# Adding lam for the large block's last stage one step ahead, in a kernel of two attention layers

## The chip, the cores and the metric

The kernel runs on one core of a Trainium2 chip. The metric is the device time of one execution in microseconds (us), from first to last instruction plus a small launch share. Engines go by their short names: PE is the matrix engine (PEld its weight load), DVE the vector engine, ACT the scalar (activation) engine, POOL the GpSimd engine, SP the engine whose queue issues the DMAs.

## The reference, cut to what matters

The input x is 8 batches of 512 tokens with 128 features. Two parts follow each other, each adding to x. Only the first part bears on this change:

```python
s = einsum(Q, K) * scale                       # 16 heads of 8 features, causal
lam = max(where(mask, s, -1e30)) + 1.0         # one lam per query and head
for _ in range(4):                             # NUM_ITER Newton steps
    d = maximum(lam - s, EPS)
    f  = sum(1/d over the mask) - 1.0
    fp = -sum(1/d**2 over the mask)
    lam = lam - f / fp
p = 1 / maximum(lam - s, EPS), masked, divided by its sum
o = p @ V                                      # then o @ Wo.T, added to x
```

So each query's lam grows in four steps, each of which passes over all its scores, and a last pass with the final lam gives the weights that multiply V. The second part is six layers of windowed attention with a feed-forward net; the change does not touch its code.

## The kernel before, in words

**Blocks and pairs.** The 512 queries of a batch are cut into four blocks of 128. Block rb sees (rb + 1) * 128 keys, and its four 32-row pieces see between that less 96 and that, so a tile has 4W - 192 columns for W = (rb + 1) * 128: 320, 832, 1344, 1856 for rb 0 to 3. Each block holds 16 heads, worked on in four groups j. Blocks go in pairs, a large one (index u = 0) and a small one (u = 1): (3, 0), then (2, 1), for each of the 8 batches; the list `work` (L384) has 16 pairs.

**Three pairs at once.** The loop over w (L391) holds a pair `before` whose lam is final, a pair `now` that is in its Newton steps, and a pair `nxt` whose scores are made. Stage w has four steps k. In each step, for u = 0 and 1:

- `attend_add(before[u], k)` (L317): POOL adds the final lam to the scores of head group k, in four instructions (L263, tile `da`, one per row piece). The tile comes from the pool `dl_p`, which has three buffers, so an add may write only when the transposes (L338) of the tile three adds earlier have read it.
- `scores(nxt[u], k)` (L237): PE makes the scores (L248) and DVE moves them into the tile `ns` of that block and group (L253). That tile has one buffer per block number and group, so DVE may write it only after the `attend_add` that read the same buffer two stages back in the pair sequence, that is `attend_add(before[u], k)`.
- `newton(now[u], k)` (L283): for the large block ACT computes ln(lam + ns) with lam as its bias (L297) and exp(-...) (L298) and DVE sums with statistics (L300). For the small block POOL adds lam first, in `add_lams(now[1])` (L275, L399), four tiles `df` of four instructions each (L263), then ACT takes ln and exp (L293, L298). A short chain on DVE (L304, L306, L308, L310, L313, L314, L315) then gives the new lam.
- `attend_weigh(before[u])` (L322): ACT takes ln (L324) and exp (L325) of the tile `da`.
- `attend_sum` of the tile weighed just ahead (L327): PE transposes it (L338), DVE applies the mask (L341, tile dT), PE multiplies with V (L350), DVE copies the sum (L354). With the last group, `attend_end` follows (L362): transposes (L366), a division (L370), a transpose (L375), an ACT copy oT (L377), a matmul (L379) and DVE's add to x (L380). After block rb 1 the batch's x is complete and `normalized_T` (L88) makes its normalized transpose: statistics (L93, L94), rstd on ACT (L96, L97), `xn` on DVE (L101, four instructions), transposes (L105), an ACT copy xT (L106).

After every second stage `project` (L190) prepares the batch after next: a `normalized_T` again (same lines, copy xnT), query, key and value projections (L196 to L214), and two POOL memsets of the value tile (L206, L207).

**What sets the order.** Every engine runs its own list of instructions strictly in order; an instruction that waits holds up all behind it on its engine. The lists are not the order of the source: a scheduler in the build step works through the program by priority (earlier in the source is higher) and by its own estimate of when operands and buffers are there, so source order is only a wish.

Of the kernel before, what the change touches and what calls it, by code (L numbers as in the profile page):

```python
# [25 lines left out]
NUM_ITER = 4  # L26
# [24 lines left out]
def tile_kernel(  # L51
# [57 lines left out]
    with ExitStack() as c1:  # L109
# [119 lines left out]
        def block(b, rb, proj):  # L229

            W = (rb + 1) * P
            return dict(
                b=b, x=xs[b], rb=rb, W=W, proj=proj, ns=[None] * 4, nkb=rb + 1,
                mn=sm.tile([P, H], F32, name="mn"), lam=sm.tile([P, H], F32, name="lam"), o4=None,
            )

        def scores(t, j):  # L237

            rb, W, (qj, kn, va) = t["rb"], t["W"], t["proj"]
            sp = sp_a if rb in (0, 3) else sp_b  # L240
            ns = t["ns"][j] = sp.tile([P, 4 * W - 6 * Q], F32, name="ns", tag=f"ns{rb}{j}")
            nv = pieces(ns, W)
            s = [ps_s.tile([P, W], F32, name="s", tag="s") for a in range(4)]
            for a in range(4):
                q0 = rb * P + a * Q
                for g in range(4):
                    rows = slice(32 * g, 32 * g + 32)
                    nc.tensor.matmul(  # L248
                        s[a][rows, 0 : keys(W, a)], lhsT=qj[rows, j, q0 : q0 + Q],
                        rhs=kn[rows, 0 : keys(W, a)], start=True, stop=True,  # L250
                    )
            for a in range(4):
                nc.vector.tensor_tensor_reduce(  # L253
                    nv[a], s[a][:, 0 : keys(W, a)], far[:, N - keys(W, a) : N],
                    1.0, 3e38, ALU.add, ALU.min, t["mn"][:, 4 * j + a : 4 * j + a + 1],
                )

        def add_lam(t, d, j):

            W = t["W"]  # L260
            for a, (o, n) in enumerate(zip(pieces(d, W), pieces(t["ns"][j], W))):
                by = t["lam"][:, 4 * j + a : 4 * j + a + 1]
                nc.gpsimd.tensor_tensor(o, n, by.to_broadcast([P, keys(W, a)]), ALU.add)  # L263

        def first_lam(t):
            lam, mn = t["lam"], t["mn"]


            nc.vector.tensor_scalar(lam, mn, -1.0, 1.0, ALU.mult, ALU.add)
            for e in (2.0**-21, -(2.0**-21)):  # L270
                nc.vector.scalar_tensor_tensor(
                    lam, mn, -1.0 - e, lam, ALU.mult, ALU.max
                )

        def add_lams(t):  # L275

            t["df"] = []
            for j in range(4):
                d = dp.tile([P, 4 * t["W"] - 6 * Q], F32, name="df", bufs=4)
                add_lam(t, d, j)  # L280
                t["df"].append(d)

        def newton(t, k):  # L283
            W, lam = t["W"], t["lam"]

            st = sm.tile([P, H, 2, 3], F32, name="stw")
            for j in range(4):
                ns = t["ns"][j]
                few = W <= 2 * P
                d = t["df"][j] if few else dp.tile([P, 4 * W - 6 * Q], F32, name="d")  # L290
                dv, nv = pieces(d, W), pieces(ns, W)
                if few:
                    nc.scalar.activation(d, d, AF.Ln)  # L293
                else:
                    for a in range(4):
                        c = 4 * j + a
                        nc.scalar.activation(dv[a], nv[a], AF.Ln, bias=lam[:, c : c + 1])  # L297
                nc.scalar.activation(d, d, AF.Exp, scale=-1.0)  # L298
                for a in range(4):
                    nc.vector.bn_stats(st[:, 4 * j + a].rearrange("p u k -> p (u k)"), dv[a])  # L300

            mean = st[:, :, :, 1]
            s1 = sm.tile([P, H, 2], F32, name="s1")
            nc.vector.tensor_tensor(s1, mean, st[:, :, :, 0], ALU.mult)  # L304
            q2 = st[:, :, :, 0]
            nc.vector.tensor_tensor(q2, s1, mean, ALU.mult)  # L306
            sw2 = sm.tile([P, H], F32, name="sw2")
            nc.vector.tensor_reduce(sw2, st[:, :, :, 0:3:2], axis=AX.XY, op=ALU.add)  # L308
            sw = sm.tile([P, H], F32, name="sw")
            nc.vector.scalar_tensor_tensor(  # L310
                sw, s1[:, :, 0], -1.0, s1[:, :, 1], ALU.add, ALU.add
            )
            nc.vector.reciprocal(sw2, sw2)  # L313
            nc.vector.tensor_tensor(sw, sw, sw2, ALU.mult)  # L314
            nc.vector.scalar_tensor_tensor(lam, sw, 0.0, lam, ALU.max, ALU.add)  # L315

        def attend_add(t, j):  # L317

            d = t["d"] = dl_p.tile([P, 4 * t["W"] - 6 * Q], F32, name="da")
            add_lam(t, d, j)  # L320

        def attend_weigh(t):  # L322
            d = t["d"]
            nc.scalar.activation(d, d, AF.Ln)  # L324
            nc.scalar.activation(d, d, AF.Exp, scale=-1.0)  # L325

        def attend_sum(t, d, j):  # L327

            nkb, W, (qj, kn, va) = t["nkb"], t["W"], t["proj"]
            if j == 0:  # L330
                t["o4"] = bt.tile([P, 4, P], F32, name="o4")
            dT = tr.tile([P, nkb, 4, P], F32, name="dT", tag="dT")
            for a in range(4):

                d0 = sum(keys(W, c) for c in range(a))
                pt = ps_t.tile([P, nkb, P], F32, name="dTp", tag="t")
                for kb in range(nkb):
                    nc.tensor.transpose(  # L338
                        pt[:, kb, :], d[:, d0 + kb * P : d0 + (kb + 1) * P], ident
                    )  # L340
                nc.vector.tensor_tensor(  # L341
                    dT[:, :, a, :], pt,
                    seen[:, a, N - W : N].rearrange("p (b c) -> p b c", c=P), ALU.mult,
                )

            po = ps_o.tile([P, 4, Q], F32, name="po")
            for kb in range(nkb):
                for g in range(4):
                    rows = slice(32 * g, 32 * g + 32)
                    nc.tensor.matmul(  # L350
                        po[rows, :, :], lhsT=va[:, kb, 4 * g + j, :],
                        rhs=dT[:, kb, :, rows], start=(kb == 0), stop=(kb == nkb - 1),
                    )
            nc.vector.tensor_copy(t["o4"][:, j, :], po.rearrange("p a q -> p (a q)"))  # L354
            if j == 3:
                attend_end(t)
                if t["rb"] == 1:
                    b, xb = t["b"], t["x"]
                    normalized_T(bt, ps_m, xb, xT[:, b, :])
                    nc.sync.dma_start(x2[b].rearrange("(c p) d -> p c d", p=P), xb)  # L360
# [29 lines left out]
        now, before, ready = [], [], None  # L390
        for w in range(len(work) + 1):  # L391
            before, now, nxt = now, nxt, []
            if w + 1 < len(work):
                b, rbs = work[w + 1]
                nxt = [block(b, rb, proj) for rb in rbs]
            for t in now:
                first_lam(t)
            for k in range(NUM_ITER):
                if now:  # L399
                    add_lams(now[1])  # L400
                for u in range(2):
                    if before:
                        attend_add(before[u], k)
                    if nxt:
                        scores(nxt[u], k)
                    if now:
                        newton(now[u], k)
                    if ready:
                        attend_sum(*ready)
                        ready = None  # L410
                    if before:
                        attend_weigh(before[u])
                        ready = (before[u], before[u]["d"], k)
            if w + 2 < len(work) and work[w + 2][1][0] == 3:
                if ready:
                    attend_sum(*ready)
                    ready = None
                proj = project(work[w + 2][0])
# [511 lines left out]
```

## Time and profile before

The page covers one execution on core 0. "The first part" below is the stretch up to about 1675 us.

| what | value |
| --- | --- |
| median of 3 runs | 5099.98 us (5099.35 to 5100.96) |
| the profiled execution, its own time | 5104.72 us |
| its span, first to last instruction | 5102.8 us (1.9 us less) |
| busy over the span | PE 83%, DVE 80%, ACT 70%, POOL 58% |
| in 400 to 500 us | PE 67.8, DVE 88.6, ACT 94.4, POOL 47.9 us busy |
| in 500 to 600 us | PE 53.4, DVE 82.8, ACT 89.4, POOL 40.2 us busy |
| POOL's adds in the first part (L263) | df x1024, 396.9 us busy; da x512, 310.7 us busy |
| mean granted PE clock | 0.891 |

Rows of the timeline read: start in us from the span's start, length in us, engine, line, operation, output tile <- input tiles, shape, how many instructions are merged into the row, and in brackets how long the engine sat idle before it and what it was waiting for. The length of a merged row runs from the first start to the last end.

### The profile page before, as it was taken

To read this page: it belongs to the slowest core of one execution; us is meant where nothing else is said; L and a number is where in the kernel's file an instruction comes from. 1 tells how busy PE (TensorE), PEld (TensorE's weight loads), DVE (VectorE), ACT (ScalarE), POOL (GpSimd) and SP (SyncE) were. 2 spreads that over 40 slices of the span, in tenths; PEclk is the share of its full clock that TensorE was granted. 3 is DMA by queue.
4 is the path that set the end of the run, shared out by engine and by line. 5 is a ranking of instruction groups with operands and counts; after the bars stand their busy time and mean duration, and the time that the engine had idled before them with its cause. 6 is when DMAs were issued, how large, how long until landed. Compare 5 with 4: busy or idle time off the path is not lost.

```text
span 5102.8 us, 163213 instructions
## 1 busy us (share of the span) xinstructions
PE 4223.2 (83%) x67981; PEld 2494.8 (49%) x67981; DVE 4081.0 (80%) x11020; ACT 3561.4 (70%) x6314; POOL 2983.0 (58%) x3828
## 2 busy tenths in 40 slices
PE   4556556556554899999999999999999999999998
PEld 1233333223232556555555555565555555556554
DVE  7789888888887877877787778877787778778775
ACT  6889999999898565666666666666666566665664
POOL 2434444444345666666666666666666666666663
PEclk7667667667665999999999999999999999999999
DMA  0000000000001323232233322332323323233232
GB/s 9 1 5 1 5 5 1 5 3 3 3 1 26 69 63 73 58 81 62 60 74 71 67 65 61 76 73 59 70 59 81 69 56 73 63 76 76 62 75 48
DMA packets 273623, 240.73 MB, mean 47 GB/s; under 512 B 47056, under 2 KB 269048, under 8 KB 272888
## 3 DMA queue, kind: packets, MB, share of 16 engines
q1 hardware_dynamic: 272888, 230.30, 20.1%
q8 instruction: 538, 8.81, 0.7%
q14 instruction: 197, 1.61, 0.1%
HBM read 21.52 MB, written 4.19 MB: 5 GB/s over the span
## 4 chain that ended last, share of the span: by engine, by line
PE 43%; DVE 30%; ACT 19%; POOL 5%; issue 2%; DMA 0%; ACTq 0%; POOLq 0%; DVEq 0%; SPq 0%
PE m L555 9%; PE po L683 6%; DVE qr L571 5%; DVE ss L561 5%; ACT d L297 5%; DVE stw L300 5%; DVE qn L563 5%; PE pT L671 4%; PE acc L711 3%; PE ptq L625 3%; ACT d L298 3%; PE pv L591 3%; POOL da L263 2%; PE gp L761 2%; PE y L782 2%; PE s L645 2%
## 5 line engine op out<-in xcount | busy, mean ns | idle before, releaser
L575 POOL TENSOR_TENSOR qn<-qn,qr 128x512 f32<-128x512 f32 x768 | 978.0, 1274 | 1048.4 <-DVE qr L571 828.1
L583 POOL TENSOR_TENSOR qn<-qn,ss 128x512 f32<-128x512 f32 x768 | 785.8, 1044 | 58.4 <-ACT ss L580 58.4
L561 DVE TENSOR_REDUCE ss<-sq 128x8 f32<-128x512 f32 x768 | 521.9, 680 | 369.7 <-ACT sq L560 369.7
L263 POOL TENSOR_TENSOR df<-ns,lam 128x32 f32<-128x32 f32 (+7 forms) x1024 | 396.9, 425 | 608.9 <-DVE lam L315 393.4
L555 PE MATMUL m<-wqkv,xs 128*128 128x512 f32 x1536 | 726.6, 595 | 2.0 <-ACT v L595 1.7
L297 ACT ACTIVATE d<-ns,lam 128x416 f32<-128x416 f32 (+7 forms) x1024 | 559.4, 615 | 65.8 <-DVE stw L300 27.7
L560 ACT ACTIVATE sq<-m 128x512 f32<-128x512 f32 x768 | 459.7, 599 | 188.5 <-PE m L555 183.8
L571 DVE TENSOR_TENSOR qr<-m,tab 128x256 f32<-128x256 f32 x1536 | 572.0, 414 | 0.0
L300 DVE BATCH_NORM_STATS2 stw<-d 128x6 f32<-128x416 f32 (+7 forms) x1024 | 514.7, 561 | 55.3 <-ACT d L298 54.7
L248 PE MATMUL s<-kn,qj 32*32 32x160 f32 (+15 forms) x4096 | 426.0, 493 | 152.0 <-DVE mn L253 136.0
L630 ACT COPY qT<-ptq 128x512 f32<-128x512 f32 x768 | 419.9, 579 | 175.3 <-PE ptq L625 175.3
L338 PE MATMUL dTp<-ident,da 128*128 128x128 f32 x1280 | 297.4, 373 | 293.7 <-issue 67.0
L563 DVE TENSOR_TENSOR qn<-m,tab 128x512 f32<-128x512 f32 x768 | 522.0, 680 | 0.0
L263 POOL TENSOR_TENSOR da<-ns,lam 128x416 f32<-128x416 f32 (+15 forms) x512 | 310.7, 639 | 321.4 <-PE dTp L338 256.3
L625 PEld LDWEIGHTS ptq<-ident,qn 128*128 128x128 f32 x3072 | 359.7, 141 | 210.8 <-issue 146.8
L683 PE MATMUL po<-v,prT 64*32 64x65 f32 x24576 | 391.9, 224 | 77.5 <-DVE pr L650 77.4
L591 PE MATMUL pv<-wqkv,xs 128*128 128x512 f32 x768 | 431.6, 644 | 0.0
L656 POOL TENSOR_TENSOR pr<-pr,nm 128x512 f32<-128x512 f32 x384 | 400.9, 1044 | 20.2 <-DVE nm L655 20.2
L711 PE MATMUL acc<-oT,wo 128*128 128x512 f32 x768 | 397.6, 599 | 15.0 <-ACT oT L705 15.0
L338 PEld LDWEIGHTS dTp<-ident,da 128*128 128x128 f32 x1280 | 199.8, 187 | 421.3 <-issue 210.1
L625 PE MATMUL ptq<-ident,qn 128*128 128x128 f32 x3072 | 399.3, 273 | 7.1 <-DVE qr L571 3.6
L683 PEld LDWEIGHTS po<-v,prT 64*32 64x32 f32 x24576 | 324.5, 105 | 157.8 <-DVE pr L650 127.1
(139 smaller groups left out, 8211.7 us busy)
## 6 DMA issues: line engine op xcount, KB each, us to landing
v<-v SPq DMA_DIRECT2D x1152, 130.0 KB
v<-v SPq DMA_DIRECT2D x384, 97.5 KB
v<-v SPq DMA_DIRECT2D x192, 65.0 KB
wqkv<-in_L_ffn_Wqkv_dram SPq DMA_DIRECT2D x24, 256.0 KB
wqkv<-in_L_ffn_Wqkv_dram SPq DMA_DIRECT2D x24, 128.0 KB
wo<-in_L_ffn_Wo_dram SPq DMA_DIRECT2D x12, 256.0 KB
xb<-in_L_attn_x_dram SPq DMA_DIRECT2D x8, 256.0 KB
x<-xb SPq DMA_DIRECT2D x8, 256.0 KB
```

The source lines that it names most:

```text
L263: nc.gpsimd.tensor_tensor(o, n, by.to_broadcast([P, keys(W, a)]), ALU.add)
L297: nc.scalar.activation(dv[a], nv[a], AF.Ln, bias=lam[:, c : c + 1])
L300: nc.vector.bn_stats(st[:, 4 * j + a].rearrange("p u k -> p (u k)"), dv[a])
L555: nc.tensor.matmul(m.rearrange("p h e -> p (h e)"), lhsT=lhsT, rhs=wqkv[:, t, :], start=True, stop=True,)
L561: nc.vector.tensor_reduce(ss[:, t, :], sq, axis=AX.X, op=ALU.add)
L563: nc.vector.tensor_tensor(qc, m, tab[:, 2 * t, c, :].unsqueeze(1).to_broadcast([P, HH, DHL]), ALU.mult)
L571: nc.vector.tensor_tensor(qr[:, :, u, :], mh[:, :, 1 - u, :], sw.unsqueeze(1).to_broadcast([P, HH, hd]), ALU.mult,)
L575: nc.gpsimd.tensor_tensor(qc, qc, qr.rearrange("p h u e -> p h (u e)"), ALU.add)
L583: nc.gpsimd.tensor_tensor(qc, qc, ss[:, t, :].unsqueeze(2).to_broadcast([P, HH, DHL]), ALU.mult)
L591: nc.tensor.matmul(pv, lhsT=lhsT, rhs=wqkv[:, 2, :], start=True, stop=True,)
L625: nc.tensor.transpose(pt[:, c * P : (c + 1) * P], g["qn"][t][:, c, 2 * p : 2 * p + 2, :].rearrange("p h e -> p (h e)"), ident,)
L683: nc.tensor.matmul(po[u * QB : (u + 1) * QB, e, c, :], lhsT=prT[rows, c, u * QB : (u + 1) * QB], rhs=g["v3"][rows, n, p, :], start=True, s ...
```

## The change

`attend_add` for the large block of the finished pair moves from the head of its step to the end of the step ahead, so that in the source it stands in front of the next `add_lams`, which needs the new lam of the Newton step just made. For the first step of a stage it moves to the end of the stage ahead, where that pair is still called `now`. The small block's `attend_add` stays. No instruction is added or dropped.

```diff
@@ -399,7 +399,7 @@
                 if now:
                     add_lams(now[1])
                 for u in range(2):
-                    if before:
+                    if before and u:
                         attend_add(before[u], k)
                     if nxt:
                         scores(nxt[u], k)
@@ -411,6 +411,12 @@
                     if before:
                         attend_weigh(before[u])
                         ready = (before[u], before[u]["d"], k)
+
+                if k + 1 < NUM_ITER:
+                    if before:
+                        attend_add(before[0], k + 1)
+                elif now:
+                    attend_add(now[0], 0)
             if w + 2 < len(work) and work[w + 2][1][0] == 3:
                 if ready:
                     attend_sum(*ready)
```

## The prediction

> **What bounds the kernel now.** I read the busy time by windows first, because the change touches the first part alone. There ACT is busy 89 to 94 us of every 100, DVE 82 to 89, POOL 40 to 50, and the pattern repeats every 201 us, one batch. ACT is nearly full, so time can only go where ACT stands still. The list of waits of ACT (engine, line, what it waited for, us in total, times, longest) names the largest:
>
> ```profile
> ACT da L324 <- POOL da L263: 41.1, 14, 4.1
> ACT d L297 <- DVE stw L300: 27.7, 19, 4.0
> ACT d L297 <- DVE lam L315: 26.9, 22, 7.0
> ```
>
> Seven of the 14 waits in the first line are 4.14 us each, and all lie at one place: the first step of a stage whose `before` is (3, 0), at 341, 542, 743, 944, 1143, 1344 and 1547 us. ACT's timeline of the fourth:
>
> ```profile
> 938.86 1.08 ACT L297 ACTIVATE d<-ns,lam 128x352 f32<-128x352 f32 x2
> 944.08 1.75 ACT L324 ACTIVATE da<-da 128x1856 f32<-128x1856 f32 x1 [4.14 <-POOL da L263]
> 945.74 0.25 ACT L377 COPY oT<-pT 128x128 f32<-128x128 f32 x1
> ...
> 949.75 1.74 ACT L325 ACTIVATE da<-da 128x1856 f32<-128x1856 f32 x1
> 951.62 0.58 ACT L106 COPY xT<-pt 128x512 f32<-128x512 f32 x1
> ```
>
> ACT ends at 939.94 and has nothing until POOL has added lam to the large block. POOL's timeline says why that is late:
>
> ```profile
> 930.39 2.00 POOL L263 TENSOR_TENSOR df<-ns,lam 128x160 f32<-128x160 f32 x4 [9.69 <-DVE stw L300]
> 934.44 5.94 POOL L263 TENSOR_TENSOR df<-ns,lam 128x160 f32<-128x160 f32 x12 [2.05 <-DVE sw L308]
> 940.35 5.64 POOL L263 TENSOR_TENSOR da<-ns,lam 128x416 f32<-128x416 f32 x9
> 945.93 0.20 POOL L206 MEMSET va<- 128x64 f32 x1
> 946.02 1.34 POOL L207 MEMSET va<- 128x1472 f32 x1
> 947.34 2.86 POOL L263 TENSOR_TENSOR da<-ns,lam 128x448 f32<-128x448 f32 x3
> 956.16 1.15 POOL L263 TENSOR_TENSOR da<-ns,lam 128x32 f32<-128x32 f32 x4 [5.97 <-PE dTp L338]
> ```
>
> From 934.44 to 950.2 POOL works without a gap, and the four instructions ACT wants (416 to 512 columns, 3.71 us) stand behind sixteen `df` that ACT first needs at 956.14 (L293). In 942.30 to 944.06 POOL works 1.76 us of 1.76, ACT 0.00, DVE 0.03, PE 0.16: there POOL alone carries the end, and the chain of work that ended last runs through it (3.71 us of POOL da, then L324, L377, L379, L380).
>
> **What the change does, by the order of the two built programs.** Set side by side, the instruction lists differ in three kinds of place, and from then on not at all (SP's list is the same; the second part is the same).
>
> (1) At the seven places above, the four large `da` now stand behind the first piece of the third `df` group, ahead of 7 of the 16. (2) In six stages with `before` = (2, 1), the fourth large `da` moves ahead of one group of four `df`. (3) In stage w = 1, the first with a `before`, `da` moves as in (1), one further `da` (three of its four pieces) moves ahead of the sixteen `df` of step 1, and ACT, DVE and PE get another order there. In all other steps the scheduler keeps the old order, since its estimate has the `da` buffer come free only later. So three quarters of what the source says does not happen.
>
> **Place (1), step by step.** Group 2 starts at 934.44 as before (its buffers are freed by L300) and a group lasts 5.94/3 = 1.98, so group 3's first piece (452 ns by its shape's row) runs 936.42 to 936.85. `da` needs its lam (L315, ended 935.40) and a buffer whose transposes ended at 915.0: both are there. It ends at 936.85 + 3.71 = 940.56 instead of 944.06, and L324 starts 3.5 earlier. The seven `df` behind it end at 944.06 instead of 940.38, 12 us ahead of ACT's first use of any group (956.14) and 17 ahead of the third group's (961). After 944.06 POOL's list is as before and so are its times: its run still ends at 950.2.
>
> What is late next: L377 (oT) needs pT, ready at 942.46 by PE's row, about when L324 ends (942.3). But pT hangs on DVE's lam chain, and that has a price here. DVE's two-input instructions are long exactly while POOL works: L315 takes 0.162 in the median, but 0.39 at 939.46 and 0.64 at 893.25, where a `da` ran; each ends with POOL's piece. With pieces of 0.88 to 1.04 us in place of 0.45 to 0.61, L310 ends at 937.74 instead of 937.37, L314 and L315 follow, and L315 ends at 940.57 instead of 939.85. So pT comes 0.72 later, at 943.2, and oT is 945.74 - 943.25 = 2.5 earlier, as are L379, L380 and L93.
>
> Then L101, which makes xn and which ACT's xT copy (L106) needs. The DVE row, with the part that POOL delays:
>
> ```profile
> 948.78 1.51 DVE L101 TENSOR_SCALAR xn<-xb,mv,rstd 128x128 f32<-128x128 f32 x1
> ...
> 948.78 2.28 DVE L101 TENSOR_SCALAR xn<-xb,mv,rstd 128x128 f32<-128x128 f32 x4
> ```
>
> The first of the four took 1.51 (the median is 0.341) and ended at 950.28, just behind POOL's last piece; the other three followed freely to 951.06. In the changed kernel L101 comes 2.5 earlier, at 946.3, into the middle of POOL's unmoved run: the memset to 947.36, then pieces to 948.26, 949.20 and 950.20. At 823.87 two such DVE instructions in a row (L269) ended one behind each of two POOL pieces, so I take one per piece: the four L101 end at 947.45, 948.35, 949.29 and 950.28. That is 951.06 - 950.28 = 0.78 earlier than before, and xT, which ACT must copy before anything else, with it. ACT is ready at 949.0 and waits. So of 3.5 us some 0.7 is left. The bounds: 0, if L101 waits for the end of POOL's run as the first one did; 2.5, if it is not held up.
>
> The Trainium skill, "SBUF — State Buffer", section "Who interferes with whom", says that a DVE instruction in a two-port mode, or one with two SBUF inputs against a GpSimd instruction that reads SBUF, contends for a shared port pair, and that whichever started first keeps it for its whole instruction. The rows agree (L101 1.51 against 0.341); read strictly, that rule speaks against this change, gives the one-per-piece count and the 0.7, while without it the sum below would have 2.5 at these places.
>
> Six of the seven places have this L101. The seventh, at 1547, has no memsets, no `project` and its L101 at 1561, when POOL is idle: L324 starts at 1543.73 instead of 1547.21, less a little for DVE's delay: 3.4.
>
> **Place (2)**: 0. `da` ends 1.1 earlier and the group 0.8 later, at 841; ACT reads them at 846.8 and 858.9. If that cover were gone the price is 0.8 a place.
>
> **Place (3).** Two rows of waste belong to it:
>
> ```profile
> 170.17 0.59 DVE L253 CUSTOM_DVE_ANT_0 ns<-s,far 128x416 f32<-128x416 f32 x1 [5.31 <-POOL da L263]
> 182.06 2.40 ACT L297 ACTIVATE d<-ns,lam 128x288 f32<-128x288 f32 x5 [6.97 <-DVE lam L315]
> ```
>
> In step 0, ACT now reaches L324 at 129.15 and waits for `da` until 131.95 (2.8), where it waited 2.28 and 1.05: +0.5 better. DVE's scores (L253) come 3.5 earlier, and so do the transposes, so the chain of step 0 ends at about 154 instead of 158.4, and L297 no longer waits its 1.44 at 151.99. In step 1 the sixteen `df` start some 3 us earlier (about 155.6 instead of 158.58), and behind them one `da` piece (1.04) instead of four (3.71) is left, so L253 starts at about 155.6 + 7.88 + 1.04 = 164.5 instead of 170.17. Of these 5.6 I count 5, since ACT's 6.97 at 182.06 waits on that chain and can give them. Bounds: 8 (with more of the 6.97), and -2, if the three pieces wait for PE's transposes, which before ended only at 161.5.
>
> **Sum**: 6 x 0.7 + 3.4 + 5 = 12.6 us. Against the profiled execution's own 5104.72 that is 5092.1. That execution is 4.7 above the median of the runs; 5099.98 - 12.6 = 5087.4 is my forecast, 0.25% faster. What is saved stays saved: the second part starts from the first part's last xT.
>
> **Rivals.**
>
> *L101 is not held up by POOL*: 6 x 2.5 + 3.4 + 5 = 23.4, 5076.6. For it: L746, of the same shape, is mostly 0.342 beside POOL. Against it: 1.51 at all six places. Chance 0.13.
>
> *L101 is held to the end of POOL's run*: place (1) gives 0, leaving 8.4, 5091.6. For it: the first L101 let one full piece pass. Against it: L269. Chance 0.17.
>
> *Stage 1 gives nothing* (its other order costs in ACT what it gains in DVE): 4.2 + 3.4 = 7.6, 5092.4. Chance 0.15. Here belongs that the change hardly does what it says.
>
> *Slower*: the moved `da` waits itself, and eleven of POOL's instructions behind it with it. If its buffer came free so late that it started after about 954 instead of 936.85, the third `df` group would pass ACT's need at about 961, and each us beyond costs a us, at seven places: from 957 on some 3 x 7 = 21, 5121. The rows speak against it: the transposes ended at 915.0, twenty us ahead. Chance 0.05.
>
> **The numbers.** My own case has 0.50; its range alone is 5083 to 5092. The range to hold 8 in 10 takes in the bounds of L101 and of stage 1: 5075 to 5097. A measurement of this kernel tells about 0.2% (10.2 us) from no change. Faster by more than that: most of my case (0.39), the free L101 (0.13), a little of the others: 0.54. Within it: 0.41. Slower: 0.05.
>
> **What would show it.** ACT's L324 at the seven places starts 3.5 earlier against the preceding L297, with under 1 us of idle left; oT some 2.5 earlier. The four L101 lie one behind each POOL piece, together about 4 us long instead of 2.28, and a new ACT wait of 1.5 to 2 us stands before L106 <- PE pt. The period of a batch falls from 201.1 to about 200.4 (198.6 if L101 is free, 201.1 if it is held to the run's end). In stage 1 the 5.31 at L253 is gone and the 6.97 at L297 falls below 3. I am wrong if the period falls by more than 2, or if a new wait of L293 on POOL `df` appears.

## The result and the profile after

The changed kernel takes 5073.9 us (median of 4 runs, 5072.8 to 5075.2) against 5100.5 (4 runs, 5099.4 to 5105.0): ratio 0.9944, 95% interval 0.9931 to 0.9958. It is 26.5 us faster. The forecast was 12.6 us, with a range that began at 5075: the sign was right and the size about half, so the time lies just outside the range.

The profiled execution took 5072.79 (span 5071.1). The two profiled executions are 31.9 apart and not 26.5, since that of before lay 4.3 above its median (5100.5) and that of after 1.1 below. In the text below the two traces are laid side by side along ACT's list, and "earlier" is how much sooner the same instruction starts in the changed kernel. 0.5 us of it is there ahead of the first change and is taken off.

The same list of ACT's waits in the first part, changed kernel (us in total, times, longest):

```profile
ACT d L297 <- DVE stw L300: 30.3, 20, 6.0
...
ACT d L297 <- DVE lam L315: 19.1, 16, 2.4
ACT da L324 <- POOL da L263: 14.8, 12, 3.8
```

The wait for `da` fell from 41.1 to 14.8 and that for lam from 26.9 to 19.1; that for statistics (`stw`) grew.

**Place (1).** ACT's timeline at the same place as before, the fourth of the seven:

```profile
924.25 1.75 ACT L324 ACTIVATE da<-da 128x1856 f32<-128x1856 f32 x1 [0.63 <-POOL da L263]
926.91 0.27 ACT L377 COPY oT<-pT 128x128 f32<-128x128 f32 x1 [0.90 <-PE pT L375]
...
930.94 1.74 ACT L325 ACTIVATE da<-da 128x1856 f32<-128x1856 f32 x1
933.57 0.58 ACT L106 COPY xT<-pt 128x512 f32<-128x512 f32 x1 [0.89 <-PE pt L105]
```

L324's wait of 4.14 is 0.63. Part of it comes back in the two lines that follow, which had no wait before: 0.90 ahead of oT and 0.89 ahead of xT. POOL's and DVE's rows there:

```profile
918.12 2.43 POOL L263 TENSOR_TENSOR df<-ns,lam 128x160 f32<-128x160 f32 x5 [2.05 <-DVE sw L308]
920.51 3.71 POOL L263 TENSOR_TENSOR da<-ns,lam 128x416 f32<-128x416 f32 x4
...
929.70 1.35 POOL L207 MEMSET va<- 128x1472 f32 x1
931.01 2.90 POOL L263 TENSOR_TENSOR da<-ns,lam 128x448 f32<-128x448 f32 x3
```
```profile
929.97 3.03 DVE L101 TENSOR_SCALAR xn<-xb,mv,rstd 128x128 f32<-128x128 f32 x4
```

The four L101 now take 3.03 us together. One by one they end at 931.12, 931.19, 932.06 and 933.00; the memset ends at 931.04, the first two of the three adds at 931.98 and 932.92. So two L101 end behind the memset and one behind each add, each time 0.07 to 0.15 us after POOL's instruction.

**Place (2).** This is where the unforeseen part begins. The kernel before, POOL, DVE, and ACT's next wait:

```profile
839.31 1.15 POOL L263 TENSOR_TENSOR df<-ns,lam 128x32 f32<-128x32 f32 x4
840.41 0.82 POOL L263 TENSOR_TENSOR da<-ns,lam 128x384 f32<-128x384 f32 x1
```
```profile
839.86 0.28 DVE L304 TENSOR_TENSOR s<-stw 128x32 f32<-128x32 f32 x1
841.27 0.46 DVE L253 CUSTOM_DVE_ANT_0 ns<-s,far 128x288 f32<-128x288 f32 x1 [1.12 <-POOL da L263]
```
```profile
843.20 0.27 ACT L377 COPY oT<-pT 128x128 f32<-128x128 f32 x1 [2.42 <-PE pT L375]
```

and the changed kernel, POOL, DVE, and ACT's next wait:

```profile
822.83 2.85 POOL L263 TENSOR_TENSOR da<-ns,lam 128x288 f32<-128x288 f32 x4
```
```profile
825.42 0.32 DVE L304 TENSOR_TENSOR s<-stw 128x32 f32<-128x32 f32 x1
825.71 0.46 DVE L253 CUSTOM_DVE_ANT_0 ns<-s,far 128x288 f32<-128x288 f32 x1
```
```profile
827.65 0.27 ACT L377 COPY oT<-pT 128x128 f32<-128x128 f32 x1 [1.07 <-PE pT L375]
```

Before, DVE's L253 wrote into a tile `ns` whose fourth add (384 columns) stood on POOL behind four `df`; it waited 1.12 us for it, although it writes the first piece. Behind it on DVE stand lam's chain (L306, L310), L370 and so pT, and at 843.20 ACT waited 2.42 us for pT. In the changed kernel the add ends at 825.68, L253 follows L304 without a gap, and ACT waits 1.07.

**Stage 1** (place (3)) in the changed kernel, POOL, DVE and ACT:

```profile
155.33 2.71 POOL L263 TENSOR_TENSOR da<-ns,lam 128x416 f32<-128x416 f32 x3 [12.03 <-PE dTp L338]
158.00 7.88 POOL L263 TENSOR_TENSOR df<-ns,lam 128x160 f32<-128x160 f32 x16
165.84 1.03 POOL L263 TENSOR_TENSOR da<-ns,lam 128x512 f32<-128x512 f32 x1
```
```profile
166.91 0.59 DVE L253 CUSTOM_DVE_ANT_0 ns<-s,far 128x416 f32<-128x416 f32 x1 [7.41 <-POOL da L263]
```
```profile
169.74 1.98 ACT L297 ACTIVATE d<-ns,lam 128x288 f32<-128x288 f32 x4 [5.95 <-DVE stw L300]
...
181.27 2.40 ACT L297 ACTIVATE d<-ns,lam 128x288 f32<-128x288 f32 x5 [1.33 <-DVE lam L315]
```

The 5.31 of L253 did not go: the fourth add stayed behind the sixteen `df`, and the wait became 7.41. ACT's 6.97 at 182.06 did fall to 1.33, but a new wait of 5.95 hangs on L253.

### The profile page after: what moved, and what is told of

Same layout as the page of the kernel before. It is cut to its first block, busy times and chain, and to the rows that moved or that the text cites. A ratio compares the mean times of both kernels' runs of the same rounds, so it can differ in the third digit from the quotient of the medians.

```text
span 5071.1 us, 163242 instructions
## 1 busy us (share of the span) xinstructions
PE 4225.2 (83%) x67981; PEld 2492.7 (49%) x67981; DVE 4091.6 (81%) x11020; ACT 3560.7 (70%) x6314; POOL 2983.4 (59%) x3828
## 4 chain that ended last, share of the span: by engine, by line
PE 42%; DVE 30%; ACT 21%; POOL 3%; issue 2%; DMA 0%; SPq 0%; ACTq 0%; POOLq 0%; DVEq 0%
PE m L561 9%; PE po L689 6%; ACT d L297 5%; DVE qr L577 5%; DVE ss L567 5%; DVE stw L300 5%; DVE qn L569 5%; ACT d L298 4%; PE pT L677 4%; PE acc L717 3%; PE ptq L631 3%; PE pv L597 3%; PE y L788 2%; PE gp L767 2%; PE s L651 2%
## 5 line engine op out<-in xcount | busy, mean ns | idle before, releaser
L297 ACT ACTIVATE d<-ns,lam 128x416 f32<-128x416 f32 (+7 forms) x1024 | 559.3, 615 | 59.9 <-DVE stw L300 30.3
L338 PE MATMUL dTp<-ident,da 128*128 128x128 f32 x1280 | 293.0, 369 | 292.8 <-issue 66.6
L338 PEld LDWEIGHTS dTp<-ident,da 128*128 128x128 f32 x1280 | 197.2, 186 | 421.0 <-issue 200.9
```

## The experiments

**Each place alone** (three kernels). `attend_add` of the large block is moved only for the pairs named; in all else its call stands at the head of the step, as before (the lines that keep it there are left out of the diff, as are the lines in between).

```diff
-                if k + 1 < NUM_ITER:
-                    if before:
-                        attend_add(before[0], k + 1)
-                elif now:
+                if k + 1 == NUM_ITER and now and w and now[0]["rb"] == 3:   # place1_only
+                if k + 1 == NUM_ITER and now and now[0]["rb"] == 2:         # place2_only
+                if k + 1 == NUM_ITER and now and not w:                     # stage1_only
                     attend_add(now[0], 0)
```

place1_only: 

> Only the moves at place (1): the large block's four adds for the first step of the seven stages with before = (3, 0) from 341 us on; place (2) and stage w = 1 are as in the kernel before, and the order on ACT, PE and DVE is that of the kernel before throughout. Theory (each place gives its own share): in the changed kernel xT came 1.74 us earlier at six places and the seventh place gave about 4.3, so 6 x 1.74 + 4.3 = 14.7, and up to 4 more from the batch's remainder that the two traces show behind xT: 5100.5 - 14.7 to 18.7 = 5082 to 5086. Rival (the gain at place (2) only arises because place (1) brings the engines there in another phase, or place (1) gives it back later): then this kernel has either nearly all of the 26.5 (5074 to 5077), or no more than the prediction's 6 x 0.7 + 3.4 = 7.6 (5093).

place2_only: 

> Only the moves at place (2): the fourth large add of the first step of the six stages with before = (2, 1) ahead of one group of four df; nothing else, and no other engine's order differs from before. Theory: DVE's L253 at 841.27 stood 1.12 us behind the end of that add, which the move takes away, and the traces show 1.6 to 2.9 us gained at each place over the following 100 us, on average 2.2: 6 x 1.1 to 6 x 2.2 = 6.6 to 13, so 5087 to 5094. Rival (the prediction's own step): 0, as ACT reads neither tile before 846.8, so 5100.

stage1_only: 

> Only the moves of place (3), stage w = 1, with its other order on ACT, PE and DVE; all later stages as before. Theory: the two traces stand 0.7 to 0.8 us apart at the end of this stage, so 5099.7. Rival (the prediction's step): 5 us, so 5095.5; if the sum of the parts is to be 26.5 with less at the other places, it would have to be here.

Measured, beside 22 runs of the kernel before (5100.1):

| kernel | median us | ratio, 95% interval | against before |
| --- | --- | --- | --- |
| place1_only | 5084.9 | 0.9971, 0.9960 to 0.9983 | -15.2 |
| place2_only | 5085.3 | 0.9971, 0.9959 to 0.9982 | -14.8 |
| stage1_only | 5104.2 | 1.0008, 0.9999 to 1.0017 | +4.1, no change within the interval |

Place (2), costed at 0, is worth as much as place (1). Each place has its share: the places add up to 30.0, and with stage 1's 4.1 to 25.9 of the measured 26.5. Stage 1 alone shows neither the 0.8 that was expected nor the rival's 5. The lists of the second kernel's instructions differ from before on POOL alone and at place (2) alone, so the order there is the whole of the cause. In place1_only's trace xT comes 1.72 earlier at each of the six places, and its time lies where it was expected. Place (2)'s 14.8 is a little over the upper end (13) of what was expected. Six waits of 1.12 us are only 6.7 of it; ACT's rows show the rest. In place2_only's trace ACT's wait for pT falls from 2.42 us to 1.16, its next wait for lam, 22 us on (865.42), from 0.80 to nothing, and one for statistics at 880.88 from 1.99 to 1.34, while one for lam at 890.51 grows from 0.29 to 0.88: 2.2 at this place.

**Whose wait is it at place (2)?** The kernel before with its old order, and one tile cut in four (left out of the diff: the two loops that read `ns` now take the four pieces from this list):

```diff
-            ns = t["ns"][j] = sp.tile([P, 4 * W - 6 * Q], F32, name="ns", tag=f"ns{rb}{j}")
-            nv = pieces(ns, W)
+            tile = lambda n, i: sp.tile([P, n], F32, name="ns", tag=f"ns{rb}{j}{i}")
+            nv = t["ns"][j] = [tile(keys(W, a), a) for a in range(4)] if rb == 2 and j == 0 else pieces(tile(4 * W - 6 * Q, ""), W)
```

> The kernel before, with one thing different: the score tile ns of block rb 2, head group 0 is four tiles, one per row piece, in place of one tile with four pieces. The order of all instructions on every engine is that of the kernel before; only L253's wait differs: its first piece needs the first add (288 columns) of the old contents and not the fourth (384 columns), which in the old order stands behind four df. Theory (the gain at place (2) is L253's wait for the fourth add): L253 starts about 1.1 us earlier than at 841.27, right behind L304, without any move on POOL, and the time falls as in the kernel with place (2) alone, within 2 us of it, some 5087 to 5094. Rival (the gain of place (2) comes from POOL's earlier add itself, through ACT or PE): no change, 5100.

Measured: 5088.0 (10 runs), ratio 0.9973, interval 0.9964 to 0.9982: 12.1 us faster, 2.7 from place2_only (2 were expected) with overlapping intervals. The order of POOL's, DVE's and ACT's instructions is that of before throughout. POOL and DVE at the place:

```profile
832.28 1.15 POOL L263 TENSOR_TENSOR df<-ns,lam 128x32 f32<-128x32 f32 x4
833.38 0.83 POOL L263 TENSOR_TENSOR da<-ns,lam 128x384 f32<-128x384 f32 x1
```
```profile
832.84 0.29 DVE L304 TENSOR_TENSOR s<-stw 128x32 f32<-128x32 f32 x1
833.05 0.44 DVE L253 CUSTOM_DVE_ANT_0 ns<-s,far 128x288 f32<-128x288 f32 x1
```

The fourth add still stands behind four `df` and ends at 834.21, but L253 starts at 833.05, ahead of that. It is 1.18 us earlier against before, as by the move on POOL (1.11). So the gain at place (2) is L253's wait for a whole tile, and POOL's order is only one way to shorten it.

**Places (1) and (2) without stage 1** (`elif now and w`, and the calls inside the stage as before).

> The moves of places (1) and (2) together, stage w = 1 as before. Theory (the places add up, as each has a wait of its own; the two parts alone took 15.2 and 14.8 us off the medians, stage 1 alone nothing that can be told from noise): 5100.1 - 30.0 = 5070, within 5 of the changed kernel's 5073.9. Rival (part of what one place gives is the same time as the other's, through a common wait later in the batch): well short of the sum, 5078 to 5085, and then stage 1 would have to give the rest in the changed kernel.

Measured: 5072.3, ratio 0.9944, 0.9930 to 0.9957, the same as the changed kernel. They add up, and stage 1 gives nothing that these runs can tell.

**What holds L101?** The changed kernel with a shorter run on POOL (the kernel leaves out three adds; in the built order the one that is left stands behind both memsets of `va`):

```diff
-        def add_lam(t, d, j):
+        def add_lam(t, d, j, few=4):
             W = t["W"]
-            for a, (o, n) in enumerate(zip(pieces(d, W), pieces(t["ns"][j], W))):
+            if few == 1: nc.gpsimd.memset(d[:, keys(W, 0) :], 1.0)
+            for a, (o, n) in enumerate(list(zip(pieces(d, W), pieces(t["ns"][j], W)))[:few]):
 ...
-            add_lam(t, d, j)
+            add_lam(t, d, j, 1 if t["rb"] == 3 and j == 1 and t["b"] > 0 else 4)
```

> The changed kernel, with POOL's run at the junction made shorter: for the large block of the pairs (3, 0) of batches 1 to 7 and head group 1, three of the four adds (448, 480 and 512 columns, 2.90 us together at 931.01) are left out and a single memset of these 1440 columns stands in for them, ahead of the two memsets of va. So these weights are not computed. The order on ACT, PE and DVE is that of the changed kernel. POOL's run then ends at about 932.3 instead of 933.92. Theory (the four L101 are held at POOL's instruction boundaries, 3.03 us from 929.97 to 933.00 where four at the median of 0.341 take 1.4): they end between 931.3 and 932.4, ACT's wait of 0.89 us ahead of the xT copy (L106) goes to 0 to 0.3, and six places give 3.5 to 5.4 us: about 5069. Rival (L101 is long for a cause that has nothing to do with POOL): L101's 3.03, the wait of 0.89 and the time of 5073.9 stay.

Measured: 5062.8 median, ratio 0.9927, 0.9915 to 0.9939; but the five executions are 5061.2 to 5063.7 and one of 5072.1, and the profile is of that one. In it:

```profile
935.00 1.35 POOL L207 MEMSET va<- 128x1472 f32 x1
936.32 0.91 POOL L263 TENSOR_TENSOR da<-ns,lam 128x416 f32<-128x416 f32 x1
```
```profile
934.86 2.71 DVE L101 TENSOR_SCALAR xn<-xb,mv,rstd 128x128 f32<-128x128 f32 x4
```
```profile
938.13 0.59 ACT L106 COPY xT<-pt 128x512 f32<-128x512 f32 x1 [0.56 <-PE pt L105]
```

Counted from L324's start, the memset now ends at 7.20 where it ended at 6.79, and the first two L101 end at 7.28 and 7.35 instead of 6.87 and 6.94; the third ends at 8.16, behind the add at 8.07. All six places show this to 0.01 us. The ends of L101 move with the ends of POOL's instructions, later as well as earlier, so POOL holds them. The expected size was missed: the boundary that the first two pass moved back, so xT is only 0.34 earlier a place (2.0 in all), not 0.6 to 0.9. Why four of the five executions are another 10 us faster this one profile cannot show; their mean granted clock was 0.896 to 0.898, that of the profiled one 0.892, so the median's 11 us are not all the shorter run's.

**What is left of L253's waits?** The changed kernel with every `ns` in four tiles (the diff above without the condition).

> The changed kernel with every score tile ns cut in four tiles, one per row piece, so that each L253 waits for the add of its own piece alone. Theory (what place (2) gained is a wait that L253 has at other places too: 46.5 us in 29 waits are left in the changed kernel's first part, up to 7.41 at 166.91): a part of them goes and some is on the path, 5055 to 5070. Rival (the remaining waits of L253 on POOL stand beside other work, and only the one at place (2) led to the end): 5071 to 5076.

Measured: 5063.5 (5061.5 to 5063.9), ratio 0.9924, 0.9911 to 0.9936, the fastest kernel with the full computation, 10 us ahead of the changed one. The gain lies in stage 1: at 230 us on before's clock it is 12.5 earlier than before where the changed kernel is 0.2. POOL, DVE and ACT in stage 1, at the instructions that waited 7.41 and 5.95:

```profile
155.54 3.71 POOL L263 TENSOR_TENSOR da<-ns,lam 128x416 f32<-128x416 f32 x4 [11.61 <-PE dTp L338]
159.21 7.90 POOL L263 TENSOR_TENSOR df<-ns,lam 128x160 f32<-128x160 f32 x16
```
```profile
159.49 0.58 DVE L253 CUSTOM_DVE_ANT_0 ns<-s,far 128x416 f32<-128x416 f32 x1
```
```profile
164.57 1.98 ACT L297 ACTIVATE d<-ns,lam 128x288 f32<-128x288 f32 x4 [0.55 <-DVE stw L300]
```

POOL's list has changed with the split: the scheduler put the fourth add ahead of the sixteen `df`, too. It ends at 159.25, before L253 starts at 159.49, so at this place L253 would not have waited for a whole tile either. The order on DVE and ACT also differs, here and further on. This run therefore shows what L253's wait costs in stage 1, but not that a smaller tile by itself removes it there; no run has this order with whole tiles.

**The move in all steps.** The scheduler left three quarters of the moves out because it saw no free `da` buffer. With rings of their own for large and small blocks it makes more of them:

```diff
-            d = t["d"] = dl_p.tile([P, 4 * t["W"] - 6 * Q], F32, name="da")
+            d = t["d"] = dl_p.tile([P, 4 * t["W"] - 6 * Q], F32, name="da", tag=f"da{t['rb'] < 2}", bufs=2)
```

> The changed kernel with the weight tiles da of the large and the small blocks in rings of their own, two buffers each in place of three shared ones: the tile that an add writes was then last read four adds ago and not three, and the scheduler does move the adds for steps 1 to 3 ahead of df, as the source says, in three quarters of the places where it did not. Theory (the same gain as at places (1) and (2): ACT and DVE stand waiting for POOL's da, 14.8 us at L324 and 46.5 at L253): 5050 to 5068. Rival (with more adds in front, the df come later and ACT waits for them at L293, now 22.3 us in 12 waits; or the engines contend more): 5074 to 5095.

Measured: 5076.4, ratio 0.9950, 0.9937 to 0.9962: no faster than the changed kernel. The rival is nearer, by another wait than it named. DVE and ACT, first part:

```profile
DVE ns L253 <- POOL da L263: 26.7, 26, 1.6
```
```profile
ACT d L297 <- DVE lam L315: 42.7, 25, 6.7
...
ACT df L293 <- POOL df L263: 19.2, 12, 2.7
```

L253's wait fell from 46.5 to 26.7, but ACT's wait for lam rose from 19.1 to 42.7; that for `df` did not rise (22.3 before that). The order on DVE and PE is another one as well, so what made the wait for lam longer stays open.

**Split tiles, with the change's parts put on one by one.** Three kernels: old order, place (1) alone, places (1) and (2). The split changes DVE's order against whole tiles at other places; between the three only POOL's order differs among POOL, DVE and ACT, and only at the places named.

split_tiles_old_order: 

> The kernel before, its POOL order too, with every score tile ns cut in four. Theory (the split takes over what place (2) gave, and frees the same wait in stage 1; place (1) has another cause and is still missing here): about 15 slower than the changed kernel with split tiles (5063.5), less what stage 1 gives or takes: 5075 to 5082. Rival (the split does the whole of what the change does, place (1) too): 5061 to 5067.

split_tiles_place1: 

> Split tiles with the moves of place (1) alone; against the kernel of the line above POOL's list differs at place (1) only, the other engines' lists not at all. Theory (with split tiles L253 no longer waits for the fourth add, so place (2) has nothing left to give): the same as split tiles with both places, within 3 us, and 13 to 16 faster than split tiles in the old order. Rival (place (2) gives its 15 us by something else than L253's wait): 12 to 15 slower than split tiles with both places.

split_tiles_places12: 

> Split tiles with the moves of places (1) and (2) and stage w = 1 in the old order. It is the pair to the run of split tiles with the whole change (5063.5), which differs by stage 1 alone. Theory (stage 1 gave nothing in the changed kernel because L253 there waited 7.41 us for the one add that stayed behind the sixteen df; with split tiles this wait does not hold the statistics behind it, so the move is worth the 5 us of the prediction): 5067 to 5070. Rival (the old order of stage 1 loses nothing once the tiles are split, as its wait of 5.31 at L253 is gone as well): 5060 to 5065.

| kernel | median us | ratio, 95% interval |
| --- | --- | --- |
| split_tiles_old_order | 5082.1 | 0.9958, 0.9945 to 0.9972 |
| split_tiles_place1 | 5074.0 | 0.9945, 0.9933 to 0.9958 |
| split_tiles_places12 | 5072.8 | 0.9940, 0.9927 to 0.9952 |
| split_tiles_all (with stage 1) | 5063.5 | 0.9924, 0.9911 to 0.9936 |

With split tiles place (2) is worth 1.2, within the scatter, where it was worth 14.8; from the third batch on the two traces run alike (197.8 to 198.0 us a batch in both, but for the last). That settles place (2). Stage 1 is worth 9.3 where it gave nothing, and split_tiles_places12 is slower than the expected 5067 to 5070. The adds that were moved ahead there are good once the fourth goes with them; in the changed kernel it stayed behind sixteen `df`, and L253 waited for it. Place (1) is worth 8.1, less than the 13 to 16 expected. xT is 1.7 earlier at each of the six places, but in the last four batches only 0.4 to 0.7 of it is left 8 us on, at ACT's kn copy (L204), and the batches are hardly shorter (197.9 us on average against 198.1 in the old order, without the last). In these batches PE's two matmuls ahead of kn (L196) take 1.63 to 1.66 us together, where they took 1.02 to 1.13; more on that at the end. In the two traces the gain comes from the first two batches (4.6 and 1.9) and from the seventh place, which has no kn and keeps 3.5, after 3.2 were lost ahead of the first, where the lists are the same.

**Split tiles for rb 3 and 0 only** (the condition is `rb in (0, 3)`).

> The changed kernel with split score tiles for the blocks rb 3 and 0 only; those of rb 2 and 1 are whole. POOL's and ACT's lists are those of split tiles for all blocks; on DVE and PE the order of the later stages is that of the changed kernel. Theory (the 8 to 10 us that split tiles gain over the changed kernel lie in stage 1, whose waits of L253 are on tiles of the pair (3, 0), while at the later batches the fourth add already stands ahead of df, so that whole tiles lose nothing): stage 1 as with all tiles split, the later batches as in the changed kernel, 194.9 and 197.5 us in turn in place of 197.9 each, so 5055 to 5063. Rival (the split also gains at the tiles of (2, 1)): slower than all split, 5064 to 5072.

Measured: 5068.4, ratio 0.9938, 0.9924 to 0.9951. Stage 1 gains its 12.6 as expected, but the later batches take 196.2 to 199.1 us, 197.6 in the mean, and not the 196.0 of the same five in the changed kernel. The expected 5055 to 5063 is missed and the time lies in the rival's range; all tiles split stays ahead, though the two intervals overlap.

## Why the prediction fell short, step by step

Held against the two traces; the last column is their difference over the whole first part.

| step of the prediction | forecast | measured |
| --- | --- | --- |
| L324 at place (1) | 3.5 earlier | 3.51, at all six |
| oT left after DVE's delayed chain | 2.5 | 2.51 |
| xT left after L101 | 0.7 x 6 = 4.2 | 1.74 x 6 = 10.4 |
| the seventh place | 3.4 | 3.5 |
| from xT on to place (2) | 0 | 4.2 (from -2.1 to +2.3 a batch) |
| place (2) and the 100 us behind it | 0 | 13.0 |
| stage 1 | 5 | 0.2 |
| sum | 12.6 | 31.3 |

**The step that failed is place (2): "ACT reads them at 846.8 and 858.9".** It asked when ACT needs the two tiles that change places, and not who else waits for the add. The same prediction had named that reader (DVE's L253 may write only after the add has read the old contents) and had used it in stage 1; at place (2) the row with 1.12 us did not enter it. Removing that wait gives 14.8 us by moving the add and 12.1 by cutting the tile, and where L253 does not wait, moving the add gives 1.2. The prediction's own sign of being wrong came true with it: the mean period of a batch, from L324 to L324, fell by 4.6 us (201.0 to 196.4) and not by 0.7; its other sign, a new wait of L293 on `df`, did not (22.6 and 22.3 us).

**L101: the mechanism was right, the size was not.** POOL's boundaries hold the four L101, but two pass behind the memset's end, where one per instruction was assumed; the run of four ends one POOL instruction earlier, so 1.74 is left instead of 0.78.

**Stage 1: the direction of the wait was wrong.** The prediction had the `df` start at 155.6 and L253 at 164.5. The trace has `da` waiting for PE's transposes until 155.33, the `df` from 158.00 (158.58 before) and L253 at 166.91. This was the condition of its lower bound ("if the three pieces wait for PE's transposes"). Where the fourth add is ahead as well, the `df` start later still (159.21), L253 starts at 159.49 and the stage is 12.5 us shorter than before; so it was the wait at L253 that held the gain, as far as these runs go.

The rival that put the gain of a free L101 at 5076.6 came near to the time by the wrong cause: L101 is not free.

## What to carry to other kernels

When an instruction moves ahead, list everyone who waits for it: who reads what it writes, and who may overwrite what it reads. As these kernels were built, a tile with one buffer lets its next writer start only when the last reader of any part is done, so the last of several readers behind unrelated work is a wait for the whole tile; cutting the tile can be worth nearly as much as reordering (12.1 against 14.8 us at place (2)), but it also lets the scheduler choose another order, so read the built one. A gain at one place holds only to the next wait, so cost it there, and expect parts to be worth more or less with other parts in place.

## What the runs showed of the hardware

**POOL holds one-input DVE instructions, too, and the order in which they pass repeats.** L101 takes 0.34 alone and 0.89 to 1.57 beside POOL, its end 0.07 to 0.15 behind an end of POOL's. Behind a memset two passed, behind an add one. The first L101 in the kernel before is an exception that no run explains: it started at 4.70 after L324, let POOL's boundary at 5.12 pass and ended behind the next, at 6.21. The Trainium skill, "SBUF — State Buffer", section "Who interferes with whom", says that a DVE tensor_scalar can run in a two-port mode, and that in such a mode DVE and GpSimd block each other for a whole instruction, whoever issues first going first. The rows agree on the blocking, though none shows the mode; the L101 that was passed over at 5.12 does not fit the order.

**Batches of the same code differ by 2.6 us with PE's clock.** In the changed kernel they take 194.9 and 197.5 us in turn. From L324 on, the first rows that differ are PE's last transposes ahead of the query projection (L338 at 740.26 and 935.25, 1.25 and 1.70 us) and that projection itself, here in the short batch and in the long one, with the busy times of PE, PEld, DVE, ACT and POOL in the same stretches and the granted clock (PEclk, the column ahead of DMA's share):

```profile
741.35 1.02 PE L196 MATMUL pq<-xnT,wT 128*128 128x512 f32 x2
```
```profile
936.74 1.91 PE L196 MATMUL pq<-xnT,wT 128*128 128x512 f32 x2
```
```profile
741.35:742.37 1.02, 1.02 (x6) 0.49 (x5) 1.02 (x3) 1.02 (x4) 0.00 (x0) 1.00 0.00 0
936.74:938.65 1.91, 1.91 (x4) 0.77 (x4) 1.27 (x4) 1.91 (x5) 0.00 (x0) 0.50 0.00 0
```

At 0.50 the two matmuls take 1.91 us instead of 1.02, kn comes 1.0 us later, L297 at 26 us another 1.0 and oT at 101 us 0.5. It is so in all six batches: 1.02 us in the short ones, 1.91 or 1.92 in the long ones. In the trace of places (1) and (2) without stage 1 the two kinds alternate the other way round, the long one first, with the same 1.02 and 1.91 or 1.92. How the granted clock falls against the batch differs from one to the next. That is likely where the scatter of the step "from xT on" comes from, a part of what the split tiles gain or lose in the later batches, and the spread of up to 11 us between executions of one kernel; no run here set the clock, so this is argued and not shown.
